# Keys and queries of layer 0 from one product of TensorE

## The chip, the cores and the metric

The kernel runs on one core of one Trainium2 chip. It is one program for five engines that run side by side and wait for each other by semaphores: TensorE (matrix products, named PE in the profile), ScalarE (ACT), VectorE (DVE), GpSimd (POOL) and SyncE (SP, which issues DMAs). The metric is the time of one execution on the device, in microseconds (us).

## The reference

The input `x` is (4, 128, 64, 64): 4 batches, 128 channels, 4096 positions. Two layers follow each other. Everything is float32.

```
# layer 0: attention over positions, with 64 channels for queries and keys
g = groupnorm(x, 32 groups)                  # per batch, as (128, 4096)
q = Wq g + bq ; k = Wk g + bk                # (64, 4096) each
v = Wv g + bv                                # (128, 4096)
x = x + v softmax(q^T k)^T                   # softmax over the keys

# layer 1, on tokens t (4096 per batch, 128 channels)
t = t + causal_attention(layernorm(t))       # 128 channels
t = t + recurrence(batchnorm(W layernorm(t)))   # y = sigmoid(wx + V y), over the tokens
```

## The kernel before, in words

All of `x` stays in SBUF as `X`, 128 channels on the partitions. A batch's 4096 positions are cut into 8 chunks of 512 columns (`QT`). The work order is by batch, in a batch by layer, in a layer by tile: one tile is one chunk of queries, 64 in all (`tiles`). A tile is cut into units; a unit takes 256 keys, as two blocks of 128 (`h` = 0 and 1). In layer 0 a tile has 16 units; in layer 1, which is causal, it has 2 (c + 1).

For a unit, `score` makes the products of two key blocks with the queries into the PSUM tile `ps` (L452), and ScalarE puts the exponential of it into `s` or, for the first unit of a tile, into `tot` (L467). `product` multiplies that with the values, into the PSUM accumulators `av` (L483), and VectorE adds `s` to the running sum `tot` (L501). The main loop issues `score(i + 1)`, then small side work (`gap` in layer 0, and `turn`, which takes a step of the first two jobs of a queue), then `product(i)`. So TensorE has one unit's score ahead of its product, and side work stands between the two.

Layer 0 has only 64 channels for keys and queries, half of the partitions. Two products with 64 rows can run in TensorE at once, on different halves of its rows. So the two blocks of a unit are computed side by side: block `h` = 0 from partitions 0 to 63, block 1 from 64 to 127. For this both keys and queries must stand on both halves. Before, this is had by doubling the weights: `wk` is `W0k` twice side by side, so that the product `pk` (L332) has all 64 key channels twice, and one copy of ScalarE with the bias (L333) puts it into `K`. The same is done with `wq` for the queries: `pq` (L344) and its copy (L346). Of the doubled `K`, each half uses every other block only.

In each batch's layer 0 the steps are these.

- `groupnorm` finds the group statistics, scales the weights with them and works out the biases: three small products into `pb` (L308).
- `feed0` makes keys and values of a chunk. In batch 0, at the start of the kernel, both go into one PSUM tile of two banks, `pkv` (of `ps_pair`, two buffers); the values come from 8 passes (L338) and a copy of ScalarE (L339). In batches 1 to 3 `pk` and `pv` are tiles of one bank each from `ps_m`, which has two buffers for all side work, and the steps are jobs in the queue, worked off during layer 1 of the batch before.
- `prep0` makes the queries of one chunk, in a tile with two buffers. For chunk 0 it is a job; for chunk c + 1 it is called in `gap` at unit 0 of tile c, so between the second score and the first product of a tile.
- `sample` finds a shift for the exponent from one block of scores (L252 to L266).
- `end` closes a tile: VectorE adds up, transposes (`zt`, L377, and `rt`, L388) and scales. At the last unit of a tile of layer 0 both accumulators are copied out of PSUM (`acc`, L495: one by ScalarE, the other by VectorE), which frees their banks for the next tile.

The order of instructions on each engine comes from a scheduler, which also puts in the semaphore waits. It keeps accesses of different engines to one PSUM tile apart. After the last tile, the recurrence is worked out (`chunks`, L617 to L656).

## Time and profile before

| | |
|---|---|
| time, median of 3 runs | 2634.52 us (2634.27 to 2634.62) |
| span of the profiled execution | 2633.1 us |
| TensorE | 2587.0 us busy, 98% |
| VectorE | 1502.3 us busy, 57% |
| ScalarE | 1116.6 us busy, 42% |
| first score product (L452) starts | 34.87 us |
| recurrence | from about 2554 us on |

In a row of a group, the tile names stand as out<-in, then the shape, the count, the busy time and the mean duration in ns, and last the idle time of the engine just before these instructions and what ended it. One fp32 product is two passes of TensorE, so counts of products are doubled. In the shape, `64*128` is a product with 64 rows, `128*128` one with all rows. In the timeline a row begins with the start in us and the time until the end of the last of its instructions. Ends of products are modelled, and successive products overlap in these rows; the distance between starts is the better measure. PEld is the load of weights into TensorE.

### The profile page before, as it was taken

To read this page: it belongs to the slowest core of one execution; us is meant where nothing else is said; L and a number is where in the kernel's file an instruction comes from. 1 tells how busy PE (TensorE), PEld (TensorE's weight loads), DVE (VectorE), ACT (ScalarE), POOL (GpSimd) and SP (SyncE) were. 2 spreads that over 40 slices of the span, in tenths; PEclk is the share of its full clock that TensorE was granted. 3 is DMA by queue.
4 is the path that set the end of the run, shared out by engine and by line. 5 is a ranking of instruction groups with operands and counts; after the bars stand their busy time and mean duration, and the time that the engine had idled before them with its cause. 6 is when DMAs were issued, how large, how long until landed. Compare 5 with 4: busy or idle time off the path is not lost.

```text
span 2633.1 us, 25672 instructions
## 1 busy us (share of the span) xinstructions
PE 2587.0 (98%) x9988; PEld 1221.3 (46%) x9988; DVE 1502.3 (57%) x2543; ACT 1116.6 (42%) x1302; POOL 99.3 (4%) x118
## 2 busy tenths in 40 slices
PE   9999999999999999999999999999999999999975
PEld 4444445444444444445444444544544444444444
DVE  3566666535556566543556565654455566655548
ACT  3444443334444443333444444333444444334345
POOL 0000000000000000000000000000000000000004
PEclk9999999999999999999999999999999999999988
DMA  3000000000000000000000000000000000100013
GB/s 135 1 1 1 1 1 12 9 4 5 5 1 1 1 1 4 13 4 8 5 1 1 1 1 1 12 9 4 5 4 1 1 1 1 68 12 4 8 68 129
DMA packets 9090, 35.74 MB, mean 14 GB/s; under 512 B 1920, under 2 KB 2688, under 8 KB 7296
## 3 DMA queue, kind: packets, MB, share of 16 engines
q1 hardware_dynamic: 8528, 33.89, 3.3%
q8 instruction: 80, 1.31, 0.2%
q14 instruction: 50, 0.41, 0.1%
q10 hardware_dynamic: 432, 0.13, 0.0%
HBM read 17.24 MB, written 16.78 MB: 13 GB/s over the span
## 4 chain that ended last, share of the span: by engine, by line
PE 97%; DVE 1%; issue 0%; ACT 0%; DMA 0%; POOL 0%; SPq 0%; ACTq 0%; POOLq 0%; DVEq 0%
PE av L483 51%; PE ps L452 34%; PE pg L617 2%; PE pq L344 1%; PE po L401 1%; PE pq L363 1%; PE pw L413 1%; PE pv L338 1%; PE pk L332 1%; PE pt L162 1%; PE pt_f L162 1%; PE pb L181 1%; PE pz L384 1%; PE pb_f L181 1%; DVE T L632 1%
## 5 line engine op out<-in xcount | busy, mean ns | idle before, releaser
L483 PE MATMUL av<-s,V 64*128 64x512 f32 (+3 forms) x4864 | 1355.9, 585 | 0.0
L467 ACT ACTIVATE s<-ps,shift 128x1024 f32<-128x1024 f32 (+4 forms) x796 | 808.5, 1024 | 1288.5 <-PE ps L452 1167.4
L501 DVE TENSOR_TENSOR tot<-tot,s 128x1024 f32<-128x1024 f32 (+4 forms) x796 | 880.4, 1111 | 793.6 <-ACT s L467 716.2
L452 PE MATMUL ps<-q,K 64*128 64x512 f32 (+4 forms) x3200 | 1026.8, 578 | 0.0
L483 PEld LDWEIGHTS av<-s,V 64*128 64x128 f32 (+1 forms) x4864 | 551.4, 188 | 610.8 <-issue 603.2
L452 PEld LDWEIGHTS ps<-q,K 64*128 64x128 f32 (+1 forms) x3200 | 414.2, 188 | 484.2 <-issue 472.6
L483 PE MATMUL av<-tot,V 64*128 64x512 f32 (+2 forms) x384 | 122.9, 605 | 0.0
L467 ACT ACTIVATE tot<-ps,shift 128x1024 f32<-128x1024 f32 (+2 forms) x68 | 71.5, 1057 | 110.1 <-PE ps L452 93.8
L156 POOL TENSOR_TENSOR rstd<-rstd,mhalf 128x4 f32<-128x4 f32 x32 | 32.2, 1007 | 1377.4 <-DVE rstd L155 1377.4
L483 PEld LDWEIGHTS av<-tot,V 64*128 64x128 f32 (+1 forms) x384 | 46.2, 187 | 55.4 <-issue 53.6
L156 POOL TENSOR_TENSOR rstd_f<-rstd_f,mhalf 128x4 f32<-128x4 f32 x32 | 32.7, 1023 | 843.5 <-DVE rstd_f L155 843.5
L175 DVE TENSOR_SCALAR V<-xt,mv,rstd 128x128 f32<-128x128 f32 x128 | 35.7, 343 | 37.9 <-POOL rstd L156 37.9
L461 DVE TENSOR_TENSOR ps<-ps,mask 128x128 f32<-128x128 f32 x128 | 38.0, 297 | 30.0 <-PE ps L452 27.7
L619 DVE SCALAR_TENSOR_TENSOR pg<-X,gain,pg 128x256 f32<-128x256 f32 x108 | 48.5, 489 | 5.7 <-PE pg L617 5.1
L175 DVE TENSOR_SCALAR rows<-xt_f,mv_f,rstd_f 128x128 f32<-128x128 f32 x128 | 36.2, 343 | 20.7 <-POOL rstd_f L156 20.7
L168 DVE BATCH_NORM_STATS2 st<-xt 128x6 f32<-128x128 f32 x128 | 27.9, 280 | 34.9 <-ACT xt L164 34.9
L402 DVE TENSOR_TENSOR X<-X,po 128x512 f32<-128x512 f32 x32 | 22.0, 688 | 43.6 <-PE po L401 43.6
L377 DVE STREAM_TRANSPOSE zt<-tot 128x512 f32<-128x512 f32 x64 | 45.5, 711 | 2.2
L388 DVE STREAM_TRANSPOSE rt<-sums 128x512 f32<-128x512 f32 x64 | 45.4, 709 | 1.5
L617 PE MATMUL pg<-Y,FV 128*128 128x256 f32 x148 | 39.2, 414 | 6.5 <-ACT Y L612 6.5
L374 DVE TENSOR_TENSOR tot<-tot 128x512 f32<-128x512 f32 x64 | 44.3, 692 | 2.1
L379 DVE TENSOR_REDUCE part<-zt 128x16 f32<-128x512 f32 x64 | 43.9, 686 | 2.2
(139 smaller groups left out, 1154.8 us busy)
## 6 DMA issues: line engine op xcount, KB each, us to landing
D<-X SPq DMA_DIRECT2D x32, 256.0 KB, 2.0
T<-D SPq DMA_DIRECT2D x4, 2048.0 KB, 7.9
X<-in_x SPq DMA_DIRECT2D x3, 2048.0 KB, 12.2
out<-T SPq DMA_DIRECT2D x2, 2048.0 KB, 7.5
out<-T SPq DMA_DIRECT2D x4, 1024.0 KB, 7.9
X<-in_x SPq DMA_DIRECT2D x4, 512.0 KB, 6.0
W0v<-in_w0v ACTq DMA_DIRECT2D x1, 64.0 KB, 5.6
W1q<-in_w1q SPq DMA_DIRECT2D x1, 64.0 KB, 1.9
```

The source lines that it names most:

```text
L156: nc.gpsimd.tensor_tensor(dst, dst, mhalf[:, :n], ALU.pow)
L162: nc.tensor.transpose(pt[:, j, :], src[:, ts(j, P)], ident)
L175: nc.vector.tensor_scalar(rows[:, j, :], xt[:, j, :], mv[:, j, 0:1], rstd[:, j : j + 1], ALU.subtract, ALU.mult)
L181: nc.tensor.transpose(pb[:, j, :], rows[:, j, :], ident)
L377: nc.vector.transpose(zt.rearrange("p j a -> p (j a)"), both)
L388: nc.vector.transpose(rt.rearrange("p (j a) -> p j a", a=R), r.unsqueeze(2).to_broadcast([P, QT // R, R]))
L452: mm = nc.tensor.matmul(ps[:, h, first[h] :], lhsT=K[layer, b][rows, ts(2 * u + h, P)], rhs=Q[t][rows, first[h] :], start=True, stop=True,)
L467: nc.scalar.activation(s[:, *a], ps[:, *a], AF.Exp, bias=shift[layer, b])
L483: nc.tensor.matmul(acc[:, first[h] :], lhsT=V[layer, b][rows, 2 * u + h, :], rhs=s[rows, h, first[h] :], start=u == 0 and h == 0, stop=u = ...
L501: nc.vector.tensor_tensor(total[:, *a], total[:, *a], s[:, *a], ALU.add)
L617: nc.tensor.matmul(ps, lhsT=FV, rhs=last[b], start=True, stop=True)
L619: nc.vector.scalar_tensor_tensor(pv, wx, gain, pv, ALU.mult, ALU.add)
```

## The change

Keys and queries of a chunk come from one product. The weights stand side by side, `W0k` and then `W0q`, 64 columns each, so that the product has the keys on partitions 0 to 63 and the queries on 64 to 127. What each half needs is put there by the copies out of PSUM: keys of even blocks to the low half and of odd blocks to the high half, queries to both. Two copies are ScalarE's, two VectorE's. `K` has then half the columns. The queries of a whole batch are kept in a tile `Q0`, and `prep0` is gone, and with it the query product between tiles. Its aim is to take 32 products off TensorE.

```diff
-            for n, w in (("k", W0k), ("v", W0v), ("q", W0q)):
+            for n, w in (("kq", W0kq.rearrange("p h o -> p (h o)")), ("v", W0v)):
...
         def feed0(b, c):
             if c == 0:
-                K[0, b] = kv.tile([P, N], F32, tag="K0", name=f"K0_{b}")
+                K[0, b] = kv.tile([P, NB // 2, P], F32, tag="K0", name=f"K0_{b}")
+                Q[0, b] = kv.tile([P, N], F32, tag="Q0", name=f"Q0_{b}")
...
-            nc.tensor.matmul(pk, lhsT=gn[b]["k"], rhs=src, start=True, stop=True)
-            nc.scalar.activation(K[0, b][:, ts(c, QT)], pk, AF.Identity, bias=gn[b]["bk"])
+            nc.tensor.matmul(pk, lhsT=gn[b]["kq"], rhs=src, start=True, stop=True)
+            bias = gn[b]["bkq"]
+            low, high = slice(0, CQ), slice(CQ, P)
+            blocks = pk.rearrange("p (u h t) -> p h u t", h=2, t=P)
+            pair = ts(c, 2)
+            nc.scalar.activation(K[0, b][low, pair, :], blocks[low, 0], AF.Identity, bias=bias[low])
+            nc.vector.tensor_scalar(K[0, b][high, pair, :], blocks[low, 1], bias[low], None, ALU.add)
+            cols = ts(c, QT)
+            nc.scalar.activation(Q[0, b][high, cols], pk[high], AF.Identity, bias=bias[high])
+            nc.vector.tensor_scalar(Q[0, b][low, cols], pk[high], bias[high], None, ALU.add)
             yield
...
-        def prep0(b, c):
-            pq = ps_m.tile([P, QT], F32, tag="m", name=f"pq0_{b}_{c}")
-            nc.tensor.matmul(pq, lhsT=gn[b]["q"], rhs=X[:, b, ts(c, QT)], start=True, stop=True)
-            Q[0, b, c] = qp.tile([P, QT], F32, tag="q0", name=f"q0_{b}_{c}")
-            nc.scalar.activation(Q[0, b, c], pq, AF.Identity, bias=gn[b]["bq"])
...
             for h in range(2):
-                rows = slice(0, P) if layer else ds(h * CQ, CQ)
+                if layer:
+                    k, q = K[1, b][:, ts(2 * u + h, P)], Q[t]
+                else:
+                    rows = ds(h * CQ, CQ)
+                    k, q = K[0, b][rows, u, :], Q[0, b][rows, ts(c, QT)]
...
-            if u == 0:
-                if c + 1 < NQ:
-                    preps[0, b, c + 1] = Job(prep0(b, c + 1))
-                    preps[0, b, c + 1].complete()
-                if norm:
-                    norm.step()
-            if u == 2 and norm:
+            if u in (0, 2) and norm:
                 norm.step()
```

With it go some smaller edits. In `groupnorm` of batch 0, one and then three warm-up products of 256 columns (`busy(1, 2)` and `busy(3, 2)`) are put where TensorE has nothing to do; the small products into `pb` are two instead of three. The tile `zt` of `end` comes from a pool with one buffer instead of two, which makes room for `Q0`. The tile `T_0`, which the recurrence needs, takes `Q0`'s place at the end instead of `K0`'s. The key and query biases are one tile `B0kq`, loaded by two DMAs instead of four.

More of the change, by code (lines that the diff above doesn't have):

```diff
@@ L96, in fast @@
         nc.sync.dma_start(out=X[:, 0, ts(h, N // 4)], in_=x[0, :, ts(h, N // 4)])
-    W0k = const.tile([P, CQ], F32, name="W0k")
+    W0kq = const.tile([P, 2, CQ], F32, name="W0kq")
     W0v = const.tile([P, C], F32, name="W0v")
-    W0q = const.tile([P, CQ], F32, name="W0q")
-    for t, src in ((W0k, w0k), (W0v, w0v), (W0q, w0q)):
+    for t, src in ((W0kq[:, 0, :], w0k), (W0v, w0v), (W0kq[:, 1, :], w0q)):
         nc.scalar.dma_start(out=t, in_=src)
-    B0q = const.tile([P, 1], F32, name="B0q")
-    B0k = const.tile([P, 1], F32, name="B0k")
-    for h in range(2):
-        nc.sync.dma_start(out=B0k[ds(h * CQ, CQ), :], in_=b0k)
-        nc.sync.dma_start(out=B0q[ds(h * CQ, CQ), :], in_=b0q)
+    B0kq = const.tile([P, 1], F32, name="B0kq")
+    nc.sync.dma_start(out=B0kq[:CQ, :], in_=b0k)
+    nc.sync.dma_start(out=B0kq[CQ:, :], in_=b0q)
     B0v = load(b0v.rearrange("o c -> c o"), [P, 1], "B0v")
@@ L205, in fast, with busy @@
         ps_m = actx.enter_context(tc.tile_pool(name="ps_m", bufs=2, space=PSUM))
-        def busy(n):
+        def busy(n, m=4):
             for k in range(n):
-                pw = ps_m.tile([P, 4, P], F32, tag="m", name=f"busy_{k}")
+                pw = ps_m.tile([P, m, P], F32, tag="m", name=f"busy_{k}")
                 nc.tensor.matmul(
-                    pw, lhsT=ones, rhs=ones.unsqueeze(1).to_broadcast([P, 4, P]), start=True, stop=True
+                    pw, lhsT=ones, rhs=ones.unsqueeze(1).to_broadcast([P, m, P]), start=True, stop=True
                 )
@@ L250, in sample @@
             rows = slice(0, P) if layer else slice(0, CQ)
+            k, q = (K[1, b][:, 0:P], Q[1, b, 0]) if layer else (K[0, b][:, 0, :], Q[0, b][:, 0:QT])
             pz = ps_m.tile([P, QT], F32, tag="m", name=f"pz_{layer}_{b}")
             nc.tensor.matmul(
-                pz, lhsT=K[layer, b][rows, 0:P], rhs=Q[layer, b, 0][rows, :], start=True, stop=True
+                pz, lhsT=k[rows, :], rhs=q[rows, :], start=True, stop=True
             )
@@ L289, in groupnorm @@
             nc.vector.tensor_tensor(dev, dev, dev, ALU.mult)
+            if b == 0:
+                busy(1, 2)
             yield
@@ L295, in groupnorm @@
             rsqrt(grs, gmv[:, 1:2], 1e-5, 1)
+            if b == 0:
+                busy(3, 2)
             yield
             got = {}
-            for n, w in (("k", W0k), ("v", W0v), ("q", W0q)):
+            for n, w in (("kq", W0kq.rearrange("p h o -> p (h o)")), ("v", W0v)):
                 got[n] = small.tile([P, P], F32, tag=f"w{n}", name=f"w{n}_{b}")
-                dst = got[n]
-                if n != "v":
-                    dst = dst.rearrange("p (h o) -> p h o", h=2)
-                    w = w.unsqueeze(1).to_broadcast([P, 2, CQ])
-                nc.vector.tensor_scalar(dst, w, grs, None, ALU.mult)
+                nc.vector.tensor_scalar(got[n], w, grs, None, ALU.mult)
             yield
-            pb = ps_m.tile([P, 3], F32, tag="m", name=f"pb_{b}")
-            for i, n in enumerate("kvq"):
+            pb = ps_m.tile([P, 2], F32, tag="m", name=f"pb_{b}")
+            for i, (n, bias) in enumerate((("kq", B0kq), ("v", B0v))):
                 nc.tensor.matmul(
@@ L310, in groupnorm @@
                 )
-            for i, (n, bias) in enumerate((("k", B0k), ("v", B0v), ("q", B0q))):
                 got["b" + n] = small.tile([P, 1], F32, tag=f"b{n}", name=f"b{n}_{b}")
@@ L317, in groupnorm @@
                 if c == 0:
-                    preps[0, b, 0] = queue(prep0(b, 0))
+                    preps[0, b, 0] = queue(sample(0, b))
             yield
@@ L340, in feed0 @@
             yield
-        def prep0(b, c):
-            pq = ps_m.tile([P, QT], F32, tag="m", name=f"pq0_{b}_{c}")
-            nc.tensor.matmul(pq, lhsT=gn[b]["q"], rhs=X[:, b, ts(c, QT)], start=True, stop=True)
-            Q[0, b, c] = qp.tile([P, QT], F32, tag="q0", name=f"q0_{b}_{c}")
-            nc.scalar.activation(Q[0, b, c], pq, AF.Identity, bias=gn[b]["bq"])
-            yield
-            if c == 0:
-                yield from sample(0, b)
         def norm1(b, c):
@@ L374, in end @@
             nc.vector.tensor_tensor(both, both, total[:, 1, :], ALU.add)
-            zt = tmp.tile([P, QT // R, R], F32, tag="zt", name=f"zt_{name}")
+            zt = one.tile([P, QT // R, R], F32, tag="zt", name=f"zt_{name}")
             nc.vector.transpose(zt.rearrange("p j a -> p (j a)"), both)
@@ L438, in score @@
                         job.complete()
+                    preps[t].complete()
                 if layer == 1:
@@ L441, in score @@
                     norms[b, c].complete()
-                if t not in preps:
-                    preps[t] = queue((prep1 if layer else prep0)(b, c))
-                preps[t].complete()
+                    if t not in preps:
+                        preps[t] = queue(prep1(b, c))
+                    preps[t].complete()
                 totals[t] = tot.tile([P, 2, QT], F32, tag="total", name=f"tot_{layer}_{b}_{c}")
@@ L450, in score @@
             for h in range(2):
-                rows = slice(0, P) if layer else ds(h * CQ, CQ)
+                if layer:
[3 more added lines that the diff above has]
+                    k, q = K[0, b][rows, u, :], Q[0, b][rows, ts(c, QT)]
                 mm = nc.tensor.matmul(
-                    ps[:, h, first[h] :], lhsT=K[layer, b][rows, ts(2 * u + h, P)],
-                    rhs=Q[t][rows, first[h] :], start=True, stop=True,
+                    ps[:, h, first[h] :], lhsT=k, rhs=q[:, first[h] :], start=True, stop=True
                 )
@@ L511, in product @@
                 if layer == 1 and c == 3 and b == B - 1:
-                    residual(0, "K0")
+                    residual(0, "Q0")
                     residual(1, "V0")
```

## The prediction

> **What bounds the kernel now.** I read the busy shares first, then the chain that ended last, then the groups kept apart by shape, and last the timeline where the change acts: the start, the place between two tiles of layer 0, and the projections of a later batch inside layer 1.

> ```profile
> PE 2587.0 (98%) x9988; PEld 1221.3 (46%) x9988; DVE 1502.3 (57%) x2543; ACT 1116.6 (42%) x1302; POOL 99.3 (4%) x118
> ...
> PE 97%; DVE 1%; issue 0%; ACT 0%; DMA 0%; POOL 0%; SPq 0%; ACTq 0%; POOLq 0%; DVEq 0%
> ```

> TensorE is busy for 98% of the span and is 97% of the chain. Outside the start and the tail, any product taken out of TensorE's queue is therefore time, unless TensorE finds nothing ready in its place. ScalarE (42%) and VectorE (57%) have room.

> ```profile
> L344 PE MATMUL pq<-X,wq 128*128 128x512 f32 x64 | 36.6, 654 | 0.0
> ...
> L418 DVE BATCH_NORM_STATS2 fstats<-pw 128x6 f32<-128x512 f32 x32 | 22.3, 695 | 23.9 <-ACT X L414 23.8
> ```

> The 32 query products appear as 64 passes (two per fp32 product). The last line matters later: the statistics only read `pw`, which ScalarE's copy also only reads, and still VectorE waited for that copy.

> The place between tile 0 and tile 1 of layer 0:

> ```profile
> 78.28 1.02 PE L452 MATMUL ps<-q,K 64*128 64x512 f32 x4
> ...
> 78.69 0.68 DVE L495 COPY acc<-av 128x512 f32<-128x512 f32 x1
> ...
> 79.24 1.13 PE L344 MATMUL pq<-X,wq 128*128 128x512 f32 x2
> ...
> 80.30 1.99 PE L483 MATMUL av<-tot,V 64*128 64x512 f32 x8
> ```

> Then tile 3 (with the query product) and tile 7 (the last one, for which there is none):

> ```profile
> 165.17 1.02 PE L452 MATMUL ps<-q,K 64*128 64x512 f32 x4
> 166.13 1.12 PE L344 MATMUL pq<-X,wq 128*128 128x512 f32 x2
> 167.09 0.60 PE L162 MATMUL pt<-ident,X 128*128 128x128 f32 x4
> 167.62 1.99 PE L483 MATMUL av<-tot,V 64*128 64x512 f32 x8
> ```

> ```profile
> 340.78 1.02 PE L452 MATMUL ps<-q,K 64*128 64x512 f32 x4
> 341.74 0.66 PE L162 MATMUL pt<-ident,X 128*128 128x128 f32 x4
> 342.32 1.99 PE L483 MATMUL av<-tot,V 64*128 64x512 f32 x8
> ```

> The start, where a value product follows the copy of its own chunk's keys:

> ```profile
> 22.79 1.02 PE L332 MATMUL pkv<-X,wk 128*128 128x512 f32 x2
> ...
> 23.85 0.69 ACT L333 ACTIVATE K<-pkv,bk 128x512 f32<-128x512 f32 x1 [0.28 <-PE pkv L332]
> ...
> 24.59 1.94 PEld L338 LDWEIGHTS pkv<-wv,X 128*128 128x128 f32 x16 [0.64 <-ACT K L333]
> ```

> The value product writes the other half of the tile `pkv`, and yet it starts 0.05 us after the key copy ended: waits are per tile.

> [...] from a 64-row product to the 128-row `pq` takes 0.96 us (78.28 to 79.24), where score to product of one mode takes 0.86 (82.12 to 82.97). [...] the granted clock is 0.66 over 15 to 20 us, and `pq` and the second `pkv` take 1.79 and 1.70 us there instead of 0.86.

> **The change part by part.**

> *Query products removed.* I took each place from the timeline.
> - Tile 0 of a batch (4): from the score's start to the first `av` it is 2.02 us in batch 0 and 2.12 in the others (660.92, 661.98, 663.04); without `pq` the two adjoin, about 0.9. That is 1.16 x 3 = 3.5. In batch 0 the first exponential (36.04 + 1.11) ends only at 37.15 and `av` starts at 37.84 now, so 0.6 there.
> - Tile 1 (4): `av` needs the banks that L495 empties. VectorE's copy (78.69 + 0.68) ends at 79.37, after the score at 79.14, so `av` can start near 79.45 instead of 80.30: 0.85 x 4 = 3.4. The query product was filler for 0.3 us here.
> - Tiles 2 to 6 (20): a transposition stands there anyway. Tile 7 shows the same place without `pq`: 1.54 us from score to `av`, against 2.45. 0.91 x 20 = 18.2. The copies end at 341.87 in tile 7, before 342.32, so no wait comes up.
> - Queries of tile 0 of batches 1 to 3, inside layer 1 (536.30 to 537.16): 0.86 x 3 = 2.6.
> - The third small product of L308: about 0.2 x 3 = 0.6.

> Sum off TensorE after the start: 3.5 + 0.6 + 3.4 + 18.2 + 2.6 + 0.6 = 28.9 us.

> *Four copies instead of two.* The chunk's bank is now read by ScalarE (keys low), VectorE (keys high), ScalarE (queries high), VectorE (queries low). In the order of the changed program each waits for the other engine: a serial chain. Prices: ScalarE 0.47 for 256 columns (the 128x256 exponentials, 473 ns) and 0.69 for 512 (L346); VectorE 0.68 for 512 (L495); for 256 columns no row has this form, and I take 0.42, between 0.30 (L461, 128 columns) and 0.68. The sum is 2.26 us, and with four hops of 0.05 about 2.5, against 0.69 for the key copy alone.

> *At the start (batch 0)* the value product waits for the whole chain, as it waited for the key copy. Two chunks go at a time: key-query products from 0 to 1.72; ScalarE keys from 1.06 to 1.53 and 1.92 to 2.39; VectorE keys from 1.58; ScalarE queries 2.39 to 3.08; VectorE queries 3.13 to 3.81; value products 3.86 to 5.8. A round takes 5.8 us. Before it took 4.33, 3.92 and 3.83 (22.79, 27.12, 31.04, 34.87). Three rounds thus lose about 2 each, some 5.9 in sum (the weight folding of layer 1 falls into the second of them). The first round held `pq` and the slow clock: it loses the chain's 2 us, but gains `pq`; the four warm-up products of 256 columns fill the gaps at 12 and 13.5 us, where TensorE waits for VectorE and GpSimd. I put it 0.6 better. The start: +5.3, with 3 and 11 as ends, since TensorE now stands for 2 of each 5.8 us and the clock can be halved again (1.7 us for one window).

> *Batches 1 to 3*, 24 chunks inside layer 1: the chain stands in ScalarE's queue ahead of the next exponential, and in VectorE's beside the running sums (1.22). A unit there is a score and a product of 1.72 each (513.49, 515.21, 516.93); with a chunk it takes 3.43 + 0.86 (key-query), and the next 3.43 + 0.97 (values). I laid one out from the end of a score product: exponential to 1.2, keys to 1.7, sum on VectorE to 2.5, keys high to 2.9, queries to 3.7, queries low to 4.5. The next score ends at 4.3, so its exponential is hardly delayed; the next key-query product wants the bank at 5.2. It fits. At diagonal units the mask comes in between, and some 0.2 shows: I take 0.5 a batch, 1.5 us in all, 0 and 8 as ends.

> *At no cost:* the single buffer of `zt` (writer and reader are both VectorE, in order); queries kept, and T_0 in Q0's place (layer 0 is over by then); fewer bias loads (the first statistics wait for x); VectorE's 32 x 1.1 us of added copies as mere work, with the engine at 57%.

> Sum: 2634.5 - 28.9 + 5.3 + 1.5 = 2612.4; I say 2612.5.

> **The rivals.**
> - *The chain is hidden at the start too.* The first round and the warm clock pay for it: 2634.5 - 28.9 = 2605.6, or 2604 with the slow window gone as well. For: `pq` and the slow clock cost 2.6 us there. Against: value products wait per tile, as the fence shows.
> - *Filler.* The query products covered waits between tiles, as the 0.3 us of tile 1. If the other 20 places gave back half, 9 us: 2621.5. Tile 7 speaks against it.
> - *The chain stops the exponentials.* If each of the 24 chunks exposes one running sum (1.22) and a hop, 31 us, with +11 at the start: 2634.5 - 28.9 + 11 + 31 = 2647.6, slower. For: both queues run in order. Against: ScalarE idles over 2 us before most exponentials there. Half of this exposure (15 us, +6 at the start) gives 2627.

> **How the numbers follow.** Forecast 0.66, hidden start 0.13, filler 0.09, partial exposure 0.07, full exposure 0.05. The range reaches from the hidden start, 2603.5, to the filler and most of a cold start, 2624. Faster by over 0.2% means below 2629.2: forecast, hidden, filler and partial exposure, 0.95; within 0.2%: 0.02; slower: 0.03, both from the full exposure.

> **What would show it.** In the profile after: no `pq<-X`; from score to `av` 0.9, 1.2 and 1.54 us in tiles 0, 1 and 2 to 7; the first score near 40 us instead of 34.87; rounds of 5.8 us at the start, with TensorE idle before value products on VectorE's query copy; in layer 1 hardly any TensorE idle on ScalarE. I am wrong if TensorE's busy share falls by more than 0.5 of a point, or if the first score stays below 37 or goes beyond 46 us.

## The result, and the profile after

The changed kernel takes 2618.76 us (2616.32 to 2619.78, 4 runs), the kernel before 2634.39 us (2632.36 to 2634.62): a ratio of 0.9941 with an interval of 0.9924 to 0.9958. It is faster by 15.6 us. The forecast was 2612.5 us, 21.9 us faster. So some 6 us are missing, and the question is where.

The page of the changed kernel, with its busy shares and its chain:

```profile
PE 2563.0 (98%) x9924; PEld 1214.7 (46%) x9924; DVE 1540.6 (59%) x2599; ACT 1111.9 (42%) x1302; POOL 99.3 (4%) x118
...
PE 96%; DVE 2%; ACT 1%; issue 1%; DMA 0%; POOL 0%; SPq 0%; ACTq 0%; POOLq 0%; DVEq 0%
```

The 64 passes of the query products are gone (9988 to 9924), and TensorE's busy time is 24.0 us less. But the span fell by only 16.2 (2633.1 to 2616.9). VectorE's share of the chain reads 2% instead of 1%.

Next the places between tiles, in the timeline of TensorE of the changed kernel, ahead of tiles 1 and 3 of layer 0 (start in us, time, engine, line, operation):

```profile
88.19 1.02 PE L455 MATMUL ps<-Q,K 64*128 64x512 f32 x4
89.55 1.99 PE L485 MATMUL av<-tot,V 64*128 64x512 f32 x8 [0.33 <-DVE acc L497]
...
173.52 1.02 PE L455 MATMUL ps<-Q,K 64*128 64x512 f32 x4
174.47 0.66 PE L159 MATMUL pt<-ident,X 128*128 128x128 f32 x4
175.06 1.99 PE L485 MATMUL av<-tot,V 64*128 64x512 f32 x8
```

From score to `av` it is 1.36 us at tile 1 of batch 0, where 2.02 stood before. The bracket says what is left there: 0.33 us of waiting for VectorE's copy of the accumulator, which the query product had covered. At tile 3 it is 1.54 instead of 2.45. This is the pattern that tile 7 had shown all along.

And the start, all engines, in the changed kernel:

```profile
14.63 1.10 PE L331 MATMUL pkv<-X,wkq 128*128 128x512 f32 x2
...
15.04 1.28 ACT L336 ACT_TABLE_LOAD   x1 [15.04 <-DVE bkq L310]
...
16.34 0.98 ACT L336 ACTIVATE K<-pkv,bkq 64x256 f32<-64x256 f32 x2
16.84 0.99 DVE L337 TENSOR_SCALAR K<-pkv,bkq 64x256 f32<-64x256 f32 x2 [0.80 <-ACT K L336]
17.35 1.26 ACT L339 ACTIVATE Q<-pkv,bkq 64x512 f32<-64x512 f32 x2
18.07 1.43 DVE L340 TENSOR_SCALAR Q<-pkv,bkq 64x512 f32<-64x512 f32 x2 [0.23 <-ACT Q L339]
18.88 1.61 PE L345 MATMUL pkv<-wv,X 128*128 128x128 f32 x8 [2.06 <-DVE Q L340]
```

The chain of four copies stands there as it was laid out: ScalarE, VectorE, ScalarE, VectorE, and only then the value product, after TensorE has waited 2.06 us. But later rounds are not what was laid out. The timeline of TensorE alone goes on like this:

```profile
31.92 1.96 PE L331 MATMUL pkv<-X,wkq 128*128 128x512 f32 x4
35.94 3.31 PE L345 MATMUL pkv<-wv,X 128*128 128x128 f32 x16 [2.06 <-DVE Q L340]
39.05 2.31 PE L331 MATMUL pkv<-X,wkq 128*128 128x512 f32 x4
43.42 2.05 PE L345 MATMUL pkv<-wv,X 128*128 128x128 f32 x16 [2.06 <-DVE Q L340]
45.40 1.99 PE L455 MATMUL ps<-Q,K 64*128 64x512 f32 x8
```

Two rows name the same 16 passes of value products, and one takes 3.31 us, the other 2.05. The stretches of the changed kernel tell why: after the stretch and its length come busy time and count of PE, PEld, DVE, ACT and POOL, then the granted clock of TensorE.

```profile
20.00:25.00 5.00, 5.00 (x15) 3.03 (x14) 0.94 (x2) 1.05 (x2) 0.00 (x0) 0.50 1.00 429
...
35.00:40.00 5.00, 4.06 (x18) 3.52 (x19) 1.43 (x2) 1.84 (x4) 0.00 (x0) 0.66 0.00 0
```

TensorE ran at half its clock for 6.8 us from 19.4 us on and for 3.4 us more from 36.5 us on, 10.2 us in all (granted clock 0.50 in both). In the start of the kernel before, it was one stretch of 3.4 us, from 16.3 us on. The first score starts at 45.40 us instead of 34.87: 10.5 us later, where 5.3 were forecast.

Setting the first `av` of every tile beside that of the kernel before gives the account of the span (us, from the two timelines):

| where | forecast | measured |
|---|---|---|
| start, to the first score | +5.3 | +10.53 |
| first score to first `av` | -0.6 | -0.63 |
| tile 0 of batches 1 to 3 | -3.5 | -3.48 |
| tile 1, four times | -3.4 | -3.17 |
| tiles 2 to 6, 20 places | -18.2 | -18.1 |
| layer 1 of batches 0 to 2 | -1.7 | -2.25 |
| after the last product | 0 | +1.0 |

Between the start and the last product every row is right to within 0.6 us. The last row is from the closing transfers: from the start of the last product to the end it is 6.5 us before and 7.5 after, and 7.2 and 7.8 in two more profiles of the changed kernel, so this row isn't put down to the change. The missing 6 us are thus 5.2 of the start and 1.0 of the tail, less 0.6 in layer 1 (tile 1 is 0.2 short).

### The profile page after: what moved, and what is told of

Its sections match the earlier page's. It is cut to its first block, busy times and chain, and to the rows that moved or that the text cites. A ratio compares the mean times of both kernels' runs of the same rounds, so it can differ in the third digit from the quotient of the medians.

```text
span 2616.9 us, 25601 instructions
## 1 busy us (share of the span) xinstructions
PE 2563.0 (98%) x9924; PEld 1214.7 (46%) x9924; DVE 1540.6 (59%) x2599; ACT 1111.9 (42%) x1302; POOL 99.3 (4%) x118
## 4 chain that ended last, share of the span: by engine, by line
PE 96%; DVE 2%; ACT 1%; issue 1%; DMA 0%; POOL 0%; SPq 0%; ACTq 0%; POOLq 0%; DVEq 0%
PE av L485 51%; PE ps L455 34%; PE pg L613 2%; PE po L399 1%; PE pq L361 1%; PE pw L411 1%; PE pv L345 1%; PE pk L331 1%; PE pt L159 1%; PE pt_f L159 1%; PE pb L178 1%; PE pz L382 1%; PE pb_f L178 1%; DVE T L628 1%; PE pkv L345 0%
## 5 line engine op out<-in xcount | busy, mean ns | idle before, releaser
L455 PE MATMUL ps<-Q,K 64*128 64x512 f32 x2048 | 525.9, 590 | 0.0
L455 PE MATMUL ps<-q,K 128*128 128x512 f32 (+3 forms) x1152 | 501.4, 557 | 0.0
L455 PEld LDWEIGHTS ps<-q,K 128*128 128x128 f32 x1152 | 216.1, 190 | 244.7 <-issue 235.7
L455 PEld LDWEIGHTS ps<-Q,K 64*128 64x128 f32 x2048 | 198.9, 187 | 238.8 <-issue 236.2
L386 DVE STREAM_TRANSPOSE rt<-sums 128x512 f32<-128x512 f32 x64 | 45.4, 709 | 1.5
```

The source lines that it names most:

```text
L386: nc.vector.transpose(rt.rearrange("p (j a) -> p j a", a=R), r.unsqueeze(2).to_broadcast([P, QT // R, R]))
L455: mm = nc.tensor.matmul(ps[:, h, first[h] :], lhsT=k, rhs=q[:, first[h] :], start=True, stop=True)
```

## The experiments

Theories for the start. A: the chain of four copies on one PSUM tile stands in front of the value products. B: the half clock has a cost of its own, beside the chain. C: the activation table, loaded at 15.04 us instead of 2.21, delays the first round. D: four copies are simply more work for ScalarE and VectorE. One experiment is for the time between tiles.

**Values not behind the copies.** In batch 0 the key-query product goes to a bank of its own, one of those that the accumulators use later; the value product keeps its tile. The copies are the same.

```diff
-                both = ps_pair.tile([P, 2, QT], F32, tag="pair", name=f"pkv_{c}")
-                pk, pv = both[:, 0, :], both[:, 1, :].rearrange("p (j d) -> p j d", j=4)
+                pk = ps_av.tile([P, QT], F32, tag=f"av{c % 2}", name=f"pk_{c}")
+                both = ps_pair.tile([P, 2, QT], F32, tag="pair", name=f"pv_{c}")
+                pv = both[:, 1, :].rearrange("p (j d) -> p j d", j=4)
```

> At the start (batch 0) the key-query product goes into one of the accumulator banks, which are free there, and the value product keeps its own tile, so that it no longer waits for the four copies of its chunk. If the serial chain of copies in front of the value product is what costs the start (my theory), TensorE has work again: the first score of layer 0 starts at 33 to 37 us instead of 45.4, and the time is 2607 to 2611 us against 2618.8. If the added copies cost as mere work on ScalarE and VectorE, or the chain binds in any place, the first score stays beyond 42 us and the time at 2616 or more. The rest of the trace should not change by more than 0.5 us.

Measured: 2609.04 us (2607.64 to 2609.50), ratio to the kernel before 0.9905 (0.9888 to 0.9921). The timeline of TensorE of this kernel:

```profile
15.23 1.10 PE L332 MATMUL pk<-X,wkq 128*128 128x512 f32 x2
16.18 0.28 PE L306 MATMUL pb<-gmv,wv 128*128 128x1 f32 x2
16.32 1.14 PE L346 MATMUL pv<-wv,X 128*128 128x128 f32 x8
...
32.22 1.12 PE L456 MATMUL ps<-Q,K 64*128 64x512 f32 x2
```

The value product follows its key-query product by 1.09 us instead of 4.25, the granted clock is 1.00 in all of the start, and the first score is at 32.22 us, a little ahead of what was expected. Since scores and the last chunk's products are mixed here, the first score flatters it: from the second tile on, TensorE is 9.55 us ahead of the changed kernel. The same copies are made by the same engines: so D falls as the main cause, and A stands. But A alone doesn't say how much of the 10.5 us is chain and how much clock, for both are gone here.

**The table load.** A one-column activation at the very start brings the table in early; nothing else is changed.

```diff
+    early = const.tile([P, 1], F32, name="early")
+    nc.scalar.activation(early, ones[:, 0:1], AF.Identity, bias=ones[:, 0:1])
```

> A one-column activation at the very start brings ScalarE's table load (1.28 us, from 15.04 to 16.32 us in the changed kernel, behind the wait for the bias) forward to where ScalarE is idle. The first key copy should then start at about 15.7 us instead of 16.34, and the first score some 0.6 us earlier, 44.8[...]. If the late table load were a large part of the 5 us that I missed, the first score would come before 43 us.

Measured: 2618.53 us (2614.19 to 2619.18), ratio 0.9935 (0.9918 to 0.9951), no gain over the changed kernel. The load is gone from there (ScalarE is busy for 2.20 us from 15 to 20 us instead of 3.48) and the first key copy starts 1.15 us after its product instead of 1.71. But the first value product still starts 4.24 us after it (4.25 in the changed kernel), since ScalarE takes the second chunk's key copy, which has to wait for that chunk's own product, ahead of the first chunk's query copy. The first score came at 47.29, with 13.7 us of half clock before it. The gain that was expected for C is a miss.

**Filler at the start.** Dummy products, read by nobody, behind the copies of every second chunk in batch 0, and in a second kernel behind every key-query product, to see whether the clock stays full with them.

```diff
             nc.vector.tensor_scalar(Q[0, b][low, cols], pk[high], bias[high], None, ALU.add)
+            if b == 0 and c % 2:
+                busy(2)
             yield
```

```diff
             nc.tensor.matmul(pk, lhsT=gn[b]["kq"], rhs=src, start=True, stop=True)
+            if b == 0:
+                busy(1 if c % 2 == 0 else 2, 2)
```

> Two products on ones, of 0.86 us each at full clock, are added after each second key-query product of the start, into banks that nobody reads; nothing else is changed. They do no work of the result[...]. If the halved clock (10.2 us of it at the start) is most of the loss, the first score comes at 38 to 41 us instead of 45.4, although 6.9 us of products are added, and the time falls by 4 to 7 us. If the chain of copies is most of it and the halved clock only runs along beside it, the first score stays within 2 us of 45.4, with a full granted clock.

> The changed kernel with dummy products of 256 columns behind each key-query product of batch 0 (one behind even chunks, two behind odd ones; read by nobody), so that TensorE has work in the gaps of the chain from the first one on. It is to part the chain from the half clock. If the clock stays full, four rounds of 6.0-6.7 us (as the three at full clock in the kernel with filler after odd chunks: 6.3, 6.7, 6.0) put the first score at 39.5-41.5 us and the time at 2612-2614.5: then the chain alone is worth some 5-6 us of the 10.5, and the half clock the other 4-5. If the half clock costs nothing of its own (copies are the limit whatever the clock), the first score stays at 44.5-46 us and the time at 2618.

Measured: 2618.14 us (2615.61 to 2618.95), ratio 0.9935 (0.9919 to 0.9952), and 2618.25 us (2616.89 to 2619.46), ratio 0.9941 (0.9925 to 0.9958). Neither kept the clock up where it was lost first: both had 6.8 us at half clock from about 20 us on (and none behind it, as in the next kernel, which has no filler), and first scores at 46.64 and 46.36. So both expectations are missed, and these two don't part chain from clock as they were meant to; filler in these places is no remedy, and its own passes stand in the queue.

**Without the warm-up products** of `groupnorm` in batch 0 (they compute nothing that is used).

```diff
-            if b == 0:
-                busy(1, 2)
...
-            if b == 0:
-                busy(3, 2)
```

> The changed kernel without the four warm-up products of 256 columns in groupnorm of batch 0 (they compute nothing that is used). Changed kernel: span 2616.9, first key-query product at 14.63 us, first score at 45.40. If these warm-ups do what they are put there for, the half clock comes earlier or longer than the 10.2 us of the changed kernel, and the first score moves to 46.5-49 us, the time to 2619.5-2622.5. If the clock at the start is set by the gaps of the chain alone, which come after them, the first score stays at 44.9-45.9 and the time within 1 us of 2618.5.

Measured: 2618.64 us (2616.89 to 2622.48), ratio 0.9949 (0.9932 to 0.9965): no difference in time from the changed kernel can be told, so the warm-up products, on which the prediction counted, aren't shown to do anything. The first score, 43.95 us, is earlier than either expectation. The profiled run had only 6.8 us of half clock, and so it shows two rounds of the same chain at full clock:

```profile
32.04 1.96 PE L327 MATMUL pkv<-X,wkq 128*128 128x512 f32 x4
36.06 2.05 PE L341 MATMUL pkv<-wv,X 128*128 128x128 f32 x16 [2.06 <-DVE Q L336]
37.95 1.96 PE L327 MATMUL pkv<-X,wkq 128*128 128x512 f32 x4
41.97 2.05 PE L341 MATMUL pkv<-wv,X 128*128 128x128 f32 x16 [2.06 <-DVE Q L336]
43.95 1.99 PE L451 MATMUL ps<-Q,K 64*128 64x512 f32 x8
```

Rounds of 5.91 and 6.00 us: the forecast's 5.8 was a figure for full clock, and there it holds.

**The changed kernel twice more,** to have the clock fall otherwise with nothing edited.

> The changed kernel itself once more, for another profile of the same program. It is to part the half clock from the chain of copies without any edit: where the clock falls in other windows, only the clock differs. If the half clock has a cost of its own, the first score comes earlier than 45.40 us when fewer than 10.2 us before it are at half clock, by about 0.4 us for each us less (nearest: 4.2 us for 10.2, from the kernel with two hand-overs at full clock, 41.23), and later when there are more. If the chain alone set the start, the first score would stay within 0.5 us of 45.40 whatever the clock.

> As the run before: the changed kernel once more. Half clock costs on its own: first score moves by about 0.4 us for each us of half clock in the start. Chain alone: 45.40 within 0.5 us whatever the clock.

Measured: one run each, 2619.41 and 2620.41 us. The timeline of TensorE in the first:

```profile
31.90 1.96 PE L331 MATMUL pkv<-X,wkq 128*128 128x512 f32 x4
35.92 2.69 PE L345 MATMUL pkv<-wv,X 128*128 128x128 f32 x16 [2.06 <-DVE Q L340]
38.41 2.96 PE L331 MATMUL pkv<-X,wkq 128*128 128x512 f32 x4
43.42 3.30 PE L345 MATMUL pkv<-wv,X 128*128 128x128 f32 x16 [2.06 <-DVE Q L340]
46.65 1.90 PE L455 MATMUL ps<-Q,K 64*128 64x512 f32 x6
```

At 43.42 us it stands where the changed kernel's first profile stood. Then a third stretch of half clock, from 43.97 us on, stretches the last value products from 2.05 to 3.30, and the first score comes 1.25 us later. Here only the clock differs, so B is shown. Together with the run without warm-up products, whose chain is the same, the four profiles lie on one line (length: first key-query product to first score; half clock: what of it lies before the first score, from the stretches):

| profile | half clock, us | length, us |
|---|---|---|
| without warm-up | 6.8 | 43.95 - 14.78 = 29.17 |
| changed kernel | 10.2 | 45.40 - 14.63 = 30.77 |
| again, first | 12.9 | 46.65 - 14.65 = 32.00 |
| again, second | 13.3 | 47.23 - 15.09 = 32.14 |

The slope is 0.47 us for each us at half clock, and at none the length would be 26.0 us (an estimate: 29.17 - 6.8 x 0.47). All four had at least 6.8, but the first round alone reaches lower: from the first to the third key-query product it takes 9.87 us in the changed kernel with 5.1 us of half clock, 9.05 without warm-up products with 3.3, and 8.51 with 2.2 in the kernel of the experiment after next, which is the same up to there. That is 0.48 for each us. The kernel with the early table lies on the line too (47.29 - 14.94 = 32.35 at 13.7), so the table load costs the changed kernel nothing. Before, the length was 34.87 - 14.95 = 19.92. So the 10.5 us are: 6.1 of chain, 4.8 of half clock (10.2 x 0.47), less 0.3 for the earlier first product. These 6.1 are net: the start before held a query product and 3.4 us of half clock of its own, about 1.6 by the same price. At full clock on both sides the new start would be some 7.7 us longer (an estimate: 26.0 - 19.92 + 1.6), and of the half clock 3.2 are new.

**Fewer hand-overs.** Both key copies on ScalarE, then both query copies on VectorE, in all batches. The bank goes from one of them to the other once instead of three times (two hand-overs in the expectations, with that to TensorE).

```diff
-            nc.vector.tensor_scalar(K[0, b][high, pair, :], blocks[low, 1], bias[low], None, ALU.add)
+            nc.scalar.activation(K[0, b][high, pair, :], blocks[low, 1], AF.Identity, bias=bias[low])
...
-            nc.scalar.activation(Q[0, b][high, cols], pk[high], AF.Identity, bias=bias[high])
+            nc.vector.tensor_scalar(Q[0, b][high, cols], pk[high], bias[high], None, ALU.add)
```

> The changed kernel with the same four copies dealt out otherwise: both key copies on ScalarE, then both query copies on VectorE, so that the bank goes from engine to engine once and not three times; value products still share the tile. Theory A (the serial chain in front of the value products, sum of four copies plus hand-overs): the sum of durations is 0.47+0.47+0.68+0.76 = 2.4 us and only two hand-overs go, so a value product starts 3.8-4.1 us after its key-query product instead of 4.24, and the first score at 43.5-45.4: time 2616.5-2618.8. If it were the hand-overs that cost the time, the rounds would fall to below 5.5 us at full clock and the first score to 38-40 us (time near 2612). If four copies as mere load of the engines were to blame: nothing changes, 45.4 us.

Measured: 2614.33 us (2611.37 to 2616.06), ratio 0.9929 (0.9913 to 0.9946). Both numbers for the start are missed: the first score is at 41.23. In the timeline of TensorE:

```profile
34.89 1.96 PE L331 MATMUL pkv<-X,wkq 128*128 128x512 f32 x4
38.61 1.13 PE L345 MATMUL pkv<-wv,X 128*128 128x128 f32 x8 [1.75 <-DVE Q L340]
40.17 1.13 PE L345 MATMUL pkv<-wv,X 128*128 128x128 f32 x8 [0.43 <-DVE Q L340]
41.23 1.99 PE L455 MATMUL ps<-Q,K 64*128 64x512 f32 x8
```

The round is 6.34 us, no shorter than 5.9 to 6.0: fewer hand-overs saved nothing here. The edit also shifts load, though: VectorE now makes all four query copies of a round, 3.1 us in a row (36.94 to 40.02), and the second chunk's value product waits 0.43 us more for the last. So it doesn't price a hand-over by itself. What made the difference to the changed kernel is that this profile had no half clock in the start at all; its length, 41.23 - 14.83 = 26.40 us, is near the 26.0 that the line gives for the other order of copies. Its other runs were 2 to 5 us longer at a lower mean clock, so the full clock wasn't certain. In layer 1 this order saves nearly 0.3 us in each of batches 0 to 2.

**A product put back between the tiles.** A dummy product of 512 columns, read by nobody, where the query product had been.

```diff
+            if u == 0 and c + 1 < NQ:
+                busy(1)
             if u in (0, 2) and norm:
```

> One product on ones of the size of the removed query product is put back between score and first product of tiles 0 to 6 of each batch of layer 0 (28 products); nobody reads it. If the change won by TensorE's own time there, they cost 4 x 1.16 + 4 x 0.85 + 20 x 0.91 = 26.2 us (0.4 less in the first tile): 2644 to 2646 us against 2618.8. If the removed products had been filler for waits, they cost less than 20 us: below 2639.

Measured: 2642.53 us (2638.18 to 2643.86), ratio 1.0027 (1.0017 to 1.0037), the span 23.0 us above that of the changed kernel. The timeline of TensorE ahead of tile 3:

```profile
173.53 1.02 PE L455 MATMUL ps<-Q,K 64*128 64x512 f32 x4
174.49 1.13 PE L208 MATMUL busy<-ones 128*128 128x512 f32 x2
175.45 0.60 PE L159 MATMUL pt<-ident,X 128*128 128x128 f32 x4
175.98 1.99 PE L485 MATMUL av<-tot,V 64*128 64x512 f32 x8
```

Score to `av` is 2.45 us again, exactly that of before. In batches 1 to 3 each place costs 1.16, 0.84 and five times 0.905 us, 6.5 a batch, which are the numbers that the change had taken away. In batch 0 it is 4.5, because two of the products, which depend on nothing, were drawn into the idle start; so the time stays below the 2644 us that were expected at least, and above the 2639 that filler would have had at most. Query products between tiles were no filler but full cost.

**The best of both.** The bank apart with the early table load, and then also with the two hand-overs.

> The kernel with the keys-and-queries product of batch 0 in a bank of its own (values not behind the copies), and with the activation table loaded early by a one-column activation. With the bank apart alone the first score is at 32.22 us and the time 2609.0. If the table load (1.28 us at 15.04) stands on the path of the first round there, the first score falls by 0.6-1.3 to 30.9-31.6 us and the time to 2607.7-2608.4; if value products fill that time, it stays within 0.2 us of 32.22 and 2609.0.

> The kernel with the bank apart and the early table load (2604.75 us, span 2602.6), and in addition both key copies on ScalarE and both query copies on VectorE, in all batches. In layer 1 the two-hand-over order saved 0.25-0.3 us in each of batches 0 to 2 (0.85 in all); at the start it gives ScalarE 1.5 us a chunk and VectorE 1.4 instead of 1.7 and 1.2, so the first score moves by no more than 1 us either way. Expected: 2603.0-2604.5 us. If copies as mere work were the bound of this start, the more even load (1.5 us a chunk instead of 1.7, 8 chunks) would give 1.6 us more: 2601.5-2602.5.

Measured: 2604.75 us (2604.32 to 2605.90), ratio 0.9892 (0.9876 to 0.9909); and 2602.40 us (2601.86 to 2603.04), ratio 0.9878 (0.9862 to 0.9895). The second is the fastest kernel here, 32 us below the kernel before. Of its last step, 0.92 us come up to the first `av` and 0.86 in layer 1; the rest of the 2.7 us between the two spans is nearly all behind the last product (7.1 and 6.3 us from its start to the end), where the changed kernel's own profiles differ by 0.6. The median, 2602.40, lies in the range that was named for copies as mere work (2601.5 to 2602.5); but 1.6 us at the start went with that, and 0.92 were gained there.

With the bank apart, the early table gains 3.4 us by the two ratios (0.9905 and 0.9892), 3.2 us of it before the second tile on the timeline. That is much more than its 1.28 and more than expected. The timeline of ScalarE with the bank apart alone:

```profile
34.44 0.47 ACT L337 ACTIVATE K<-pk,bkq 64x256 f32<-64x256 f32 x1 [0.82 <-PE pk L332]
35.49 1.11 ACT L470 ACTIVATE tot<-ps,shift 128x1024 f32<-128x1024 f32 x1 [0.58 <-PE ps L456]
36.63 0.68 ACT L340 ACTIVATE Q<-pk,bkq 64x512 f32<-64x512 f32 x1
```

and with the early table:

```profile
33.15 0.68 ACT L342 ACTIVATE Q<-pk,bkq 64x512 f32<-64x512 f32 x1 [0.36 <-DVE K L340]
33.86 1.11 ACT L472 ACTIVATE tot<-ps,shift 128x1024 f32<-128x1024 f32 x1
```

In the first the query copy of the last chunk is behind the first exponential, in the second ahead of it. The accumulators use the same banks as these copies: with the bank apart alone `av` waits 0.47 us for VectorE's query copy (to 38.25), and with the early table its wait is for the exponential (1.06 us, to 35.02). So the same 1.28 us are hidden behind the chain in one kernel and on the path in the other. That the order of these two explains what goes beyond 1.28 us is read from the timelines; no run changes the order alone.

## Why the prediction was right or wrong

*Query products off TensorE.* The mechanism is right, and so is nearly every part of the sum: 1.16, 0.85 and 0.91 a place were forecast, and 1.16, 0.84 (0.65 in batch 0) and 0.90 came, and the dummy product costs the same when put back. The rival of the filler falls. Only tile 1 of batch 0 is short by 0.2 us. That a product of 0.86 us gives 1.16 where both neighbours have 64 rows, and 0.90 where a transposition with 128 rows stands there anyway, fits the changes between the two shapes that go with it: in the kernel before, from the last pass of the score over `pq` to the first of `av` the starts lie 0.52 to 0.53 us apart (78.72, 79.24, 79.77, 80.30), and from `pq` to the transposition of the same shape 0.43 (166.66 to 167.09), as in successive steps within one shape.

*Batches 1 to 3 in layer 1.* The mechanism is right, and the price was somewhat high: -2.25 us instead of -1.7. The timeline of the changed kernel shows a chunk there:

```profile
523.16 0.47 ACT L336 ACTIVATE K<-pk,bkq 64x256 f32<-64x256 f32 x1
...
525.15 0.48 DVE L337 TENSOR_SCALAR K<-pk,bkq 64x256 f32<-64x256 f32 x1
...
525.66 0.68 ACT L339 ACTIVATE Q<-pk,bkq 64x512 f32<-64x512 f32 x1 [2.03 <-DVE K L337]
...
526.48 1.11 ACT L469 ACTIVATE s<-ps,shift 128x1024 f32<-128x1024 f32 x1
...
527.91 0.76 DVE L340 TENSOR_SCALAR Q<-pk,bkq 64x512 f32<-64x512 f32 x1
```

From the first copy to the end of the last it is 5.5 us, for VectorE has statistics of 0.87 and more ahead of the key copy. But the exponential comes 0.1 us after its score product is done, and layer 1 as a whole gained. The rival in which the chain stops the exponentials falls.

*The copies.* VectorE's were priced 0.42 and 0.68 us and took 0.48 and 0.755. The chain sums to 2.4 us without hops instead of 2.26. This is a small term.

*The start.* Here a term of the sum was missed: the half clock. The chain in front of the value products was right, and so was about its size: 5.9 to 6.0 us a round at full clock against 5.8, and 5.8 us in sum (6.1 less 0.3) against 5.3. The working is less exact than this sounds: 5.8 less the three rounds before (4.33, 3.92 and 3.83) is 5.3 in sum and not 5.9, the rest being an allowance for the weight folding that isn't worked out. The half clock was named, with 1.7 us for one window, which is half of the one stretch of 3.4 us in the trace of the kernel before (by the slope measured here: 3.4 x 0.47 = 1.6), but only for the upper end of 11. The forecast itself held none: it even took the window of the kernel before as gone, as its first round loses 2 us to the chain and wins the 2.6 of `pq` and the slow clock, the 0.6 better. In truth there were three windows, 4.8 us. That the clock was at risk could be read from the kernel before: its half clock followed 3.41 us in which TensorE was busy for 1.97 (12.91 to 16.32). How many windows it would be could not: the same program had three in one profile and four in two. The rival of a hidden start falls as well.

The signs that were given for being wrong didn't come in the first profile: TensorE's busy share fell by 0.3 of a point, and the first score at 45.40 us is below 46. In the two further profiles of the same program it is 46.65 and 47.23, past that bound, by half clock alone. So that this sign stayed away was in part luck.

## What to carry to other kernels

Waits that left TensorE standing went together with two costs here: the wait itself (2.06 us in a round of about 6), and half clock for the work behind it (10.2 us of it in one profile, none with the bank apart), at 0.47 us for each us; price both, the second as a range. Where two products share a PSUM tile, this scheduler put every reader of the one ahead of the other (the value product came 4.25 us after its key-query product, and 1.09 with a bank of its own), so a change that adds readers should give the second product its own bank. And a cost that is hidden behind a wait, as the table load of 1.28 us was here, appears when the wait is taken away: do both in one step.
